# Plain fp32 matmuls in place of three fp32r products, in a chain of four attention layers

## The chip, the core and the metric

The kernel runs on one core of a Trainium2 chip. The metric is the device time of one execution in microseconds (us); the time before is the median of three runs.

## The reference

The input x and a context have 32 batches of 64 tokens (rows) by 256. Four blocks follow each other, all in fp32:

```python
# layer 0: softmax over the 256 columns, 8 heads, contraction over the 64 rows
xn  = (x - mean) * rsqrt(var + eps) * gamma + beta          # per batch
out = x + Wo @ attention(Wq @ xn, Wkv @ context) + bo
# layer 1: 16 heads of 16, keys and values from layernorm(context), queries from x
x   = x + tanh(gate) * (attention(x @ Wq.T, a @ Wk.T, a @ Wv.T) @ Wo.T)
# layer 2: queries from x, keys and values from [context, x]; 128 keys
h   = rmsnorm(attention(x @ q_w + q_b, [ctx, x] @ kv_w + kv_b) @ out_w + out_b + x, w)
x   = x + gelu(h @ mlp_w1 + mlp_b1) @ mlp_w2 + mlp_b2        # 256 -> 1024 -> 256
# layer 3: self attention, cross attention with the context, MLP, each after a layernorm
x   = x + attention(ln(x) @ w_qkv + b_qkv, mask) @ w_ao + b_ao
x   = x + attention(ln(x) @ w_q + b_q, ctx @ w_kv + b_kv, mask) @ w_co + b_co
x   = x + gelu(ln(x) @ w1 + b1) @ w2 + b2
```

## The kernel before

**Layer 0** is a loop of 64 iterations (a pair of batches and two heads each), written out by hand: scores `sc`, softmax, transposes `pt`, values `av`. TensorE works here on row-tiled and column-tiled plain fp32 matmuls; its weights are folded beforehand and no projection of the kind below occurs. At fixed places of an iteration `fill` (line 1138) puts in instructions from lists that `chain` (1128) has recorded: constants, masks, the preparation of weights (`load_unit`, 503), and at the end `boot_steps` (1415), which does the first projections of layer 1 for two groups and the operands of a third. `fill` takes from a list only while the iteration's allowance for the engine lasts, and `boot_steps` is recorded once layer 1's weight units are through. Lists that are not empty when the loop ends are run out after it.

**Layers 1 to 3** work on groups of four batches (256 tokens as two tiles of 128), eight groups. In the code they are l = 0 to 3, since layer 3's self and cross attention count separately. For each group a layer has steps: normalise (`ln_stats`, `ln_apply`), turn to features by tokens (`to_fm`, 907), keys (`k_out`), values (`v_out`), queries (`fm_out`), attention in sets of 128 tokens (`attend`, 1388, with `a_scores` to `a_fin`), output projection (`out_add`), and the MLP (`mlp_steps`, 1279). Each step has a due time. All instructions are recorded, and then the class `Plan` orders them: `cost` (194) gives each instruction a time, `order` (289) is a list scheduler that starts, engine by engine, what can start first by those costs, with due times and a seeded random number for ties. The result fixes the order on each engine: TensorE (T), VectorE (V), ScalarE (A), GpSimd (G) and SyncE's DMA queue (S). The profile therefore shows nearly all instructions of layers 1 to 3 on line 125 (where the plan writes them) and those of layer 0 on line 156; tiles tell them apart.

**The split products.** A projection multiplies 256 features by 256 columns. Weights and operands are kept as two fp32r tiles each, a high part (the value cast to fp32r) and a low part (value minus high part). `terms` (925) lists the products; `proj_f` (928) and `proj_t` (934) issue them, with the weights or the tokens stationary:

```python
    def terms(w, x):
        return [(w[0], x[0], k) for k in range(2)] + [(w[0], x[1], k) for k in range(2)] + [(w[1], x[0], k) for k in range(2)]
```

So one 128x128 by 256 term takes three fp32r matmuls. The names in the profile: `xTh` and `xTl` are high and low parts of a turned operand, with a letter behind for its use (`a` tiles that `boot_steps` uses too, `o` attention output, `h` MLP hidden, `n` MLP input); `w` is a prepared weight, `wraw` and parts of `boot` are raw weights, `u` the gelu's output. Who makes them: `to_fm` casts the transposes on ScalarE and subtracts on VectorE; the MLP's hidden tile goes gelu to `u`, cast on ScalarE, subtraction on VectorE; `a_fin` (1089) makes attention output, in layer 3 with a multiplication on VectorE, a cast on ScalarE and a subtraction on GpSimd; context tiles are loaded raw (`ctx_steps`, 1229), cast on ScalarE, subtracted on GpSimd; `load_unit` loads a raw weight by DMA, scales its rows on GpSimd where a norm's scale is folded in, casts on ScalarE and subtracts on GpSimd (in a few cases VectorE).

A split weight takes twice the room, so there are 14 slots and layer 3's weights go into slots whose earlier weights are through; `load_at` (1576) says at which attention set each load comes. The bias rows (`bias_row`, 544) are the one place with plain fp32 matmuls on the whole array and 256 columns (tile `bb`).

Of the kernel before, what the change touches and what calls it, by code (L numbers as in the profile page):

```python
# [10 lines left out]
F32R = mybir.dt.float32r  # L11
# [15 lines left out]
NW = 12  # L27
NE = 3
BIG = 1.0e30


def f32(ap):
    return ap.bitcast(F32) if ap.dtype == F32R else ap

# [59 lines left out]
class Plan:  # L94
# [5 lines left out]
    SEED, TIE = 4, 0.5  # L100
# [93 lines left out]
    def cost(self, o):  # L194
# [4 lines left out]
        if o.key == "T":  # L199
            if o.method == "transpose":  # L200
                return 0.11, 0.25, (1, 1)
            l, r = ins[0], ins[1]
            k_, m_ = l.shape[0], self.size(l)
            rows = 4 if k_ <= 32 else 2 if k_ <= 64 else 1
            cols = 4 if m_ <= 32 else 2 if m_ <= 64 else 1
            n_ = self.size(r)
            if l.dtype == F32:
                return max(n_ * 1.67e-3, 0.1 if rows * cols == 1 else 0) / (rows * cols), 0.3, (rows, cols)
            return max(n_ * 0.418e-3, 0.12 if rows * cols == 1 else 0) / (rows * cols), 0.25, (rows, cols)
# [199 lines left out]
def mk_kernel(ctx: ExitStack, tc: tile.TileContext, a: dict, out: bass.AP):  # L409
# [16 lines left out]
    wraw = pool("wraw", 2)  # L426
# [13 lines left out]
    def wt(shape, dt, tag, bufs=2):  # L440
        if cur["boot"]:
            if tag == "kfm":
                return boot[:, 1024:1536].rearrange("p (k t) -> p k t", t=P)
            if cur["second"] == 2 and tag in ahead:
                return plan.tile(cur["w"], "w", shape, dt, tag, nm(tag), 2)
            o = {"xTh": 0, "xTl": 512, "qfm": 1536 - 512 * cur["second"], "craw": 2048, "z": 2048}.get(tag)
            if o is None:
                return plan.lazy(lambda: small.tile(shape, dt, tag=tag + "b", name=nm(tag), bufs=1), shape, dt)
            v = (bootx if dt == F32R else boot)[:, o:o + 512]
            return v.rearrange("p (k t) -> p k t", k=2)  # L450
        return plan.tile(cur["w"], "w", shape, dt, tag, nm(tag), bufs)
# [37 lines left out]
    ahead = {t: [ct([P, 2, D], F32R, f"{t}a{i}") for i in range(2)] for t in ("xTh", "xTl")}  # L489
    wraws = [t.rearrange("p (k n) -> p k n", k=2) for t in (boot[:, 1024:1536], boot[:, 1536:2048])]  # L490
    cur["raws"], cur["rawn"] = 2, 0
# [7 lines left out]
    def split(hi, lo, src):  # L499
        V.tensor_copy(hi, src)  # L500
        V.tensor_tensor(lo, src, f32(hi), ALU.subtract)

    def load_unit(w, key, slot, ap, rows=None, mul=None, biases=(), then=None):

        cur["rawn"] += 1
        if cur["raws"] == 2 or cur["rawn"] % 2:
            raw = plan.tile(wraw, "r", [P, 2, D], F32, "wraw", nm("wraw"), 2)
        else:
            raw = wraws[cur["rawn"] // 2 % (cur["raws"] - 2)]
        SY.dma_start(raw, ap.rearrange("(k p) n -> p k n", p=P))  # L510
        yield
        for fn in biases:
            fn(raw)
        t = plan.tile(wpool if slot < NW else cur["w"], "ww", [P, 2, 2, D], F32R, f"w{slot}", nm("w"), 1)
        if rows is not None:
            for k in range(2):
                G.tensor_scalar(raw[:, k], raw[:, k], rows[:, k:k + 1], None, ALU.mult)
        elif mul is not None:
            G.tensor_scalar(raw, raw, mul, None, ALU.mult)
        A.copy(t[:, 0], raw)  # L520
        (V if slot < 4 and plan.on else G).tensor_tensor(t[:, 1], raw, f32(t[:, 0]), ALU.subtract)
        w[key] = (t[:, 0], t[:, 1])
        if then:
            then()
        yield
# [67 lines left out]
    bootx = c0([P, 1024], F32R, "bootx")  # L593
# [75 lines left out]
    def weights1(w):  # L669
        return [load_unit(w, "k", 0, a["L1_WkT"], rows=g1, biases=[bias_f(bk1, vec("L1_ln_beta"))]),  # L670
                load_unit(w, "v", 1, a["L1_WvT"], rows=g1, biases=[bias_f(bv1, vec("L1_ln_beta"))]),
                load_unit(w, "q", 2, a["L1_WqT"], mul=0.25),
# [3 lines left out]
    def weights2(w):  # L676
        return [load_unit(w, "k", 4, a["L2_wk"]), load_unit(w, "v", 5, a["L2_wv"]),
                load_unit(w, "q", 6, a["L2_q_w"], mul=1.0 / 16, then=lambda: G.tensor_scalar(bq2, vec("L2_q_b"), 1.0 / 16, None, ALU.mult)),
                load_unit(w, "o", 7, a["L2_out_w"], biases=[bias_row(row2, vec("L2_bv"), a["L2_out_b"])])]

    def weights2m(w):
        return [load_unit(w, f"1{j}", 8 + j, a["L2_mlp_w1"][:, j * D:(j + 1) * D], rows=vec("L2_postnorm_w")) for j in range(4)] + \
               [load_unit(w, f"2{j}", (12, 13, 2, 3)[j], a["L2_mlp_w2"][j * D:(j + 1) * D], then=(lambda: spread_row(row2m, a["L2_mlp_b2"])) if j == 0 else None)
# [4 lines left out]
    s1q, s2q = ct([P, 2], F32, "s1q"), ct([P, 2], F32, "s2q")  # L688

    def quarter(dst, src):  # L690
        G.tensor_scalar(dst, src, 0.25, None, ALU.mult)
        return dst

    def weights3s(w):
        return [load_unit(w, "k", 0, a["L3_wk"], rows=s1, biases=[bias_f(bk3, sb1, vec("L3_bk"))]),
                load_unit(w, "v", 1, a["L3_wv"], rows=s1, biases=[bias_f(bv3, sb1, vec("L3_bv"))]),
                load_unit(w, "q", 4, a["L3_wq"], rows=quarter(s1q, s1), biases=[bias_f(bq3, sb1, vec("L3_bq"))],
                          then=lambda: V.tensor_scalar(bq3, bq3, 0.25, None, ALU.mult)),
                load_unit(w, "o", 6, a["L3_w_ao"], biases=[bias_row(row3a, bv3, a["L3_b_ao"])])]

    def weights3c(w):
        return [load_unit(w, "k", 5, a["L3_wkc"]), load_unit(w, "v", 7, a["L3_wvc"]),
                load_unit(w, "q", 8, a["L3_w_q"], rows=quarter(s2q, vec("L3_ln2_s")), biases=[bias_f(bq3c, vec("L3_ln2_b"), vec("L3_b_q"))],
                          then=lambda: V.tensor_scalar(bq3c, bq3c, 0.25, None, ALU.mult)),
                load_unit(w, "o", 9, a["L3_w_co"], biases=[bias_row(row3c, vec("L3_bvc"), a["L3_b_co"])])]

    def weights3m(w):
        return [load_unit(w, f"1{j}", 10 + j, a["L3_w1"][:, j * D:(j + 1) * D], rows=vec("L3_ln3_s"),
                          biases=[bias_f(b13[:, 2 * j:2 * j + 2], vec("L3_ln3_b"), vec("L3_b1")[:, 2 * j:2 * j + 2])]) for j in range(4)] + \
               [load_unit(w, f"2{j}", j, a["L3_w2"][j * D:(j + 1) * D], then=(lambda: spread_row(row3m, a["L3_b2"])) if j == 0 else None)  # L710
# [196 lines left out]
    def to_fm(x, tag=""):  # L907
# [5 lines left out]
        hi, lo = fm_tiles(tag)  # L913
        hf, lf = hi.rearrange("p k t -> p (k t)"), lo.rearrange("p k t -> p (k t)")
        A.copy(hf, p_)
        V.tensor_tensor(lf, p_, f32(hf), ALU.subtract)
        return (hi, lo)

    def fm_tiles(t=""):
        n = {"": 4, "o": 2, "h": 2, "n": 1}[t]  # L920
        hi = wt([P, 2, D], F32R, "xTh" + t, n)
        lo = wt([P, 2, D], F32R, "xTl" + t, n)
        return hi, lo

    def terms(w, x):
        return [(w[0], x[0], k) for k in range(2)] + [(w[0], x[1], k) for k in range(2)] + [(w[1], x[0], k) for k in range(2)]

    def proj_f(w, x, oc, p_):

        tt = terms(w, x)  # L930
        for i, (ww, xx, k) in enumerate(tt):
            mm(p_, ww[:, k, oc * P:(oc + 1) * P], xx[:, k, :], i == 0, i == len(tt) - 1)

    def proj_t(w, x, i, p_, first=True, last=True):

        tt = terms(w, x)
        for j, (ww, xx, k) in enumerate(tt):
            mm(p_, xx[:, k, i * P:(i + 1) * P], ww[:, k, :], first and j == 0, last and j == len(tt) - 1)

    def fm_out(w, x, tag, bias=None):  # L940
# [4 lines left out]
        for oc in range(2):  # L945
            put(o[:, oc], p_[:, oc * D:(oc + 1) * D], bias and bias[:, oc:oc + 1])
        return o

    def put(d, s_, bias):
        if bias is None:  # L950
            A.copy(d, s_)
        else:
            A.activation(d, s_, AF.Identity, bias=bias)
# [135 lines left out]
    def a_fin(u):  # L1089
        st, i = u["st"], u["i"]  # L1090
        if i == 0 and u["s"] == 0:
            st["o"] = fm_tiles("o")
        o_ = u["at"]
        c = slice(u["s"], u["s"] + 1) if u["two"] else slice(0, 2)
        hv, lv = [t[:, c, i * P:(i + 1) * P] for t in st["o"]]
        ov = o_[:, 0:D].rearrange("p (c t) -> p c t", c=2)[:, c]
        if u["kind"] == "k":
            A.copy(hv, ov)
            V.tensor_tensor(lv, ov, f32(hv), ALU.subtract)
        else:  # L1100
            rb = wt([P, 2, P], F32, "rb", 2)
            A.copy(rb.rearrange("p c t -> p (c t)"), o_[:, D:2 * D])
            V.tensor_tensor(rb, ov, rb, ALU.mult)
            A.copy(hv, rb)
            G.tensor_tensor(lv, rb, f32(hv), ALU.subtract)
# [123 lines left out]
    def ctx_steps(l, g, due, src=()):  # L1229
# [3 lines left out]
        def fetch():  # L1233
            st["raw"] = wt([P, 2, D], F32, "craw", 1)
            SY.dma_start(st["raw"], a["ctxT"][:, g * D:(g + 1) * D].rearrange("(k p) t -> p k t", p=P))

        def split_():
            hi, lo = fm_tiles()
            A.copy(hi, st["raw"])
            G.tensor_tensor(lo, st["raw"], f32(hi), ALU.subtract)  # L1240
            st["c"] = (hi, lo)
        step(n + "a", due - 2, fetch, *src)
        step(n, due, split_, n + "a")
# [21 lines left out]
    def query_step(l, g, key, w, bias, row, due):  # L1265
        st = grp[l, g]

        def fn():
            st["q"] = fm_out(w["q"], st[key], "qfm", bias)
# [9 lines left out]
    def mlp_steps(l, g, w, b1, row, key, dues, out_=None):  # L1279
# [3 lines left out]
        def up(j):  # L1283
# [5 lines left out]
            t = wt([P, 2, D], F32, "u", 3)  # L1289
            for c in range(2):  # L1290
                A.activation(t[:, c], p_[:, c * D:(c + 1) * D], AF.Gelu_apprx_tanh, bias=b1[:, j * 2 + c:j * 2 + c + 1])
            st[f"h{j}"] = fm_tiles("h")
            hh, hl = st[f"h{j}"]
            A.copy(hh, t)
            V.tensor_tensor(hl, t, f32(hh), ALU.subtract)
# [20 lines left out]
    for l in range(4):  # L1316
        for g in range(NG):
# [8 lines left out]
            elif l == 1:  # L1326
# [6 lines left out]
                query_step(l, g, "x", w2, bq2, None, f - 2)  # L1333
# [117 lines left out]
    for k in range(NP + 2):  # L1451
# [4 lines left out]
        if k == 2:  # L1456
# [3 lines left out]
            later = weights2m(w2)  # L1460
            units += later[:4]
# [106 lines left out]
    for t, tiles in ahead.items():  # L1568
        tiles += [cur["w"].tile([P, 2, D], F32R, tag=f"{t}_{i}", name=f"{t}_{i}", bufs=1) for i in range(2)]
# [11 lines left out]
    load_at(7, later[4:6])  # L1581
    load_at(16, later[6:7])
    load_at(22, later[7:])
# [10 lines left out]
    for n in range(NS):  # L1594
        if n == 4:
            cur["raws"] = 4
# [73 lines left out]
```

## Time and profile before

| | |
|---|---|
| median of three runs | 1142.94 us (1140.23 to 1143.46) |
| the profiled execution | 1139.34 us |
| its span, first to last instruction | 1137.6 us |
| mean granted TensorE clock | 0.98 |
| instructions | 35727 |
| HBM | 26.30 MB read, 2.10 MB written, 25 GB/s over the span |

Times are microseconds. PE is TensorE's matmuls and PEld its weight loads, which overlap them; DVE is VectorE, ACT ScalarE, POOL GpSimd, SP SyncE, which issues DMAs. The ends of matmuls are modelled and overlap, so how fast they follow each other is read from their starts. A group line has: source line, engine, operation, tile written and tiles read, shapes, number of instructions, busy time, mean ns of one, then the idle time of the engine before them and what ended it. A wait is put down to the releaser that came last.

### The profile page before, as it was taken

Reading aid. Unit: us, or ns where it says so; the run is one execution under the profiler, and the core shown is the slowest. Engines: PE = TensorE matmul, PEld = TensorE weight load, DVE = VectorE, ACT = ScalarE, POOL = GpSimd, SP = SyncE. Lnnn points to the kernel's source line nnn. Section 1 sums busy time; section 2 is a strip of 40 time slices with the busy share of each in tenths; the row PEclk is TensorE's granted clock in tenths of the full one; section 3 lists DMA queues with packets and bytes.
Section 4 is the critical chain, followed back from the end, with each engine's and each line's share of the span. In section 5 each row is a group of like instructions: output and inputs, shape, how many; then the busy total and the mean of one; then the engine's idle time right before and its main releaser. Section 6 shows DMA issues by size and latency. Waiting matters only on the chain.

```text
span 1137.6 us, 35727 instructions
## 1 busy us (share of the span) xinstructions
PE 1064.6 (94%) x14396; PEld 872.7 (77%) x14396; DVE 861.2 (76%) x1485; ACT 909.2 (80%) x2326; POOL 783.1 (69%) x919
## 2 busy tenths in 40 slices
PE   6999999999999996699999999999999989889998
PEld 4666666666666664588988989998998868779998
DVE  3778888787888872678788977777878888777842
ACT  2888888888888984477778888889898787878974
POOL 3789888888888864546545554457866999996520
PEclk9999999999999998799999999999999998989999
DMA  3001111111011000211211100001000111110000
GB/s 96 20 24 39 41 38 34 34 34 35 27 37 33 26 20 29 88 49 39 79 51 44 36 27 28 22 11 39 21 20 20 48 51 51 42 33 22 11 20 29
DMA packets 41301, 41.22 MB, mean 36 GB/s; under 512 B 7059, under 2 KB 37796, under 8 KB 41136
## 3 DMA queue, kind: packets, MB, share of 16 engines
q1 hardware_dynamic: 40816, 38.54, 10.9%
q8 instruction: 114, 1.87, 0.7%
q10 hardware_dynamic: 320, 0.40, 0.1%
q14 instruction: 51, 0.42, 0.1%
HBM read 26.30 MB, written 2.10 MB: 25 GB/s over the span
## 4 chain that ended last, share of the span: by engine, by line
PE 42%; POOL 8%; DVE 5%; ACT 2%; issue 1%; DVEq 0%; POOLq 0%; ACTq 0%
PE pj L125 39%; PE s L125 4%; POOL E L125 3%; DVE E L125 2%; DVE mx L125 1%; POOL xTlo L125 1%; POOL xTl L125 1%; ACT PTe L125 1%; DVE sm L125 1%; POOL boot L125 1%; POOL w L125 1%; POOL x L125 1%; POOL wraw L125 0%; ACT L125 0%; POOL rstda L125 0%
## 5 line engine op out<-in xcount | busy, mean ns | idle before, releaser
L156 POOL TENSOR_TENSOR E<-E,rs 128x512 f32<-128x512 f32 x256 | 263.2, 1042 | 51.7 <-DVE rs L156 46.7
L156 ACT ACTIVATE E<-sc,mx 128x256 f32<-128x256 f32 x512 | 237.9, 479 | 11.8 <-DVE rs L156 11.1
L156 DVE TENSOR_REDUCE mx<-sc 128x4 f32<-128x1024 f32 x128 | 156.3, 1221 | 6.6 <-PE sc L156 2.6
L156 PE MATMUL sc<-cd,T 64*128 64x256 f32 x1024 | 143.7, 400 | 11.7 <-ACT E L156 11.1
L125 POOL TENSOR_TENSOR E<-E,sm 128x512 f32<-128x512 f32 x96 | 101.2, 1079 | 68.5 <-DVE sm L125 55.8
L156 PE MATMUL av<-PT,us 128*64 128x256 f32 x1024 | 125.2, 385 | 0.3 <-DVE PT L156 0.3
L156 PEld LDWEIGHTS av<-PT,us 128*64 128x64 f32 x1024 | 68.1, 136 | 60.3 <-issue 21.0
L156 PEld LDWEIGHTS pt<-ident,E 64*128 64x128 f32 x2048 | 83.3, 139 | 37.4 <-POOL E L156 20.1
L156 PEld LDWEIGHTS sc<-cd,T 64*128 64x128 f32 x1024 | 89.2, 189 | 27.7 <-ACT E L156 19.8
L125 DVE TENSOR_REDUCE sm<-E 128x16 f32<-128x1024 f32 (+1 forms) x80 | 96.0, 1200 | 16.1 <-ACT E L125 16.0
L156 ACT ACTIVATION_READ_ACCUMULATOR E<-sc,mx 128x1 f32 x512 | 106.7, 208 | 0.0
L125 ACT COPY PTe<-pj 128x512 f32<-128x512 f32 x160 | 88.0, 590 | 17.7 <-PE pj L125 15.6
L125 PE MATMUL pj<-ident,E 128*128 128x128 f32 x640 | 90.3, 279 | 9.0 <-ACT E L125 3.2
L156 PE MATMUL pt<-ident,E 64*128 64x64 f32 x2048 | 94.7, 227 | 3.3 <-ACT PT L156 1.0
L125 PE MATMUL pj<-w,xThh 128*128 128x256 f32 x512 | 93.4, 287 | 0.1
L156 DVE COPY PT<-pt 128x512 f32<-128x512 f32 x128 | 86.7, 678 | 8.5 <-PE pt L156 7.8
L156 ACT COPY PT<-pt 128x512 f32<-128x512 f32 x128 | 75.3, 588 | 22.2 <-PE pt L156 21.0
L125 PE MATMUL pj<-xThn,w 128*128 128x256 f32 x512 | 92.3, 286 | 0.7 <-DVE rb L125 0.4
L156 DVE RECIPROCAL rs<-sm 128x2 f32<-128x2 f32 x256 | 40.7, 159 | 64.3 <-ACT E L156 60.1
L125 ACT ACTIVATE E<-E 128x1024 f32<-128x1024 f32 x80 | 84.9, 1062 | 5.4 <-DVE E L125 4.2
L125 PEld LDWEIGHTS pj<-ident,E 128*128 128x128 f32 x640 | 71.0, 142 | 17.7 <-ACT E L125 3.7
L125 DVE TENSOR_TENSOR xTlh<-u,xThh 128x512 fp32r<-128x512 f32 x64 | 54.2, 850 | 30.5 <-ACT xThh L125 30.2
(229 smaller groups left out, 2782.5 us busy)
## 6 DMA issues: line engine op xcount, KB each, us to landing
kb<-kfm SPq DMA_DIRECT2D x44, 128.0 KB, 2.0
xd<-in_x SPq DMA_DIRECT2D x32, 128.0 KB, 2.9
cd<-in_ctx SPq DMA_DIRECT2D x32, 128.0 KB, 2.7
boot<-in_ctxT SPq DMA_DIRECT2D x16, 256.0 KB, 2.9
kb<-kfm SPq DMA_DIRECT2D x64, 64.0 KB, 1.9
xt<-in_x SPq DMA_DIRECT2D x16, 128.0 KB, 2.0
boot<-in_ctx SPq DMA_DIRECT2D x8, 256.0 KB, 2.7
out<-x SPq DMA_DIRECT2D x8, 256.0 KB, 2.1
```

The source lines that it names most:

```text
L125: getattr(self.engines[o.key], o.method)(*[real(x) for x in o.p], **{k: real(x) for k, x in o.k.items()})
L156: return f(*p, **k)
```

## The change

Weights and operands stay plain fp32. `proj_f` and `proj_t` issue one fp32 matmul for each term; high and low parts, their casts and subtractions, and the raw tiles are gone. Scalings that were folded into weights (1/4 and 1/16 for the queries) move to the activation that evicts the queries. `to_fm` copies on VectorE. All weights have slots of their own; layer 2's eight MLP units are all prepared in layer 0's chains, so its four later loads go. Operand tiles get more buffers, the softmax tile `E` four in place of three. The planner's costs for matmuls and its seed change, so that the order on every engine is another.

```diff
-NW = 12
-NE = 3
+NE = 4
...
-    SEED, TIE = 4, 0.5
+    SEED, TIE = 0, 0.5
...
-            if l.dtype == F32:
-                return max(n_ * 1.67e-3, 0.1 if rows * cols == 1 else 0) / (rows * cols), 0.3, (rows, cols)
-            return max(n_ * 0.418e-3, 0.12 if rows * cols == 1 else 0) / (rows * cols), 0.25, (rows, cols)
+            if rows * cols == 1:
+                return max(n_ * (0.85e-3 if l.dtype == F32 else 0.418e-3), 0.11), 0.3, (1, 1)
+            return n_ * (1.3e-3 if l.dtype == F32 else 0.418e-3) / (rows * cols), 0.3, (rows, cols)
...
-    def load_unit(w, key, slot, ap, rows=None, mul=None, biases=(), then=None):
-
-        cur["rawn"] += 1
-        if cur["raws"] == 2 or cur["rawn"] % 2:
-            raw = plan.tile(wraw, "r", [P, 2, D], F32, "wraw", nm("wraw"), 2)
-        else:
-            raw = wraws[cur["rawn"] // 2 % (cur["raws"] - 2)]
-        SY.dma_start(raw, ap.rearrange("(k p) n -> p k n", p=P))
+    def load_unit(w, key, slot, ap, rows=None, biases=(), then=None):
+
+        t = plan.tile(wpool if slot < 24 else cur["w"], "ww", [P, 2, D], F32, f"w{slot}", nm("w"), 1)
+        SY.dma_start(t, ap.rearrange("(k p) n -> p k n", p=P))
         yield
...
-        A.copy(t[:, 0], raw)
-        (V if slot < 4 and plan.on else G).tensor_tensor(t[:, 1], raw, f32(t[:, 0]), ALU.subtract)
-        w[key] = (t[:, 0], t[:, 1])
+        w[key] = t
...
-        hi, lo = fm_tiles(tag)
-        hf, lf = hi.rearrange("p k t -> p (k t)"), lo.rearrange("p k t -> p (k t)")
-        A.copy(hf, p_)
-        V.tensor_tensor(lf, p_, f32(hf), ALU.subtract)
-        return (hi, lo)
+        t = fm_tile(tag)
+        V.tensor_copy(t.rearrange("p k t -> p (k t)"), p_)
+        return t
+
+    def fm_tile(t=""):
+        return wt([P, 2, D], F32, "xT" + t, {"": 5, "o": 3, "h": 4, "n": 2}[t])
...
     def proj_f(w, x, oc, p_):
 
-        tt = terms(w, x)
-        for i, (ww, xx, k) in enumerate(tt):
-            mm(p_, ww[:, k, oc * P:(oc + 1) * P], xx[:, k, :], i == 0, i == len(tt) - 1)
+        for k in range(2):
+            mm(p_, w[:, k, oc * P:(oc + 1) * P], x[:, k, :], k == 0, k == 1)
...
         if u["kind"] == "k":
-            A.copy(hv, ov)
-            V.tensor_tensor(lv, ov, f32(hv), ALU.subtract)
+            A.copy(to, ov)
         else:
             rb = wt([P, 2, P], F32, "rb", 2)
             A.copy(rb.rearrange("p c t -> p (c t)"), o_[:, D:2 * D])
-            V.tensor_tensor(rb, ov, rb, ALU.mult)
-            A.copy(hv, rb)
-            G.tensor_tensor(lv, rb, f32(hv), ALU.subtract)
+            V.tensor_tensor(to, ov, rb, ALU.mult)
...
         def fetch():
-            st["raw"] = wt([P, 2, D], F32, "craw", 1)
-            SY.dma_start(st["raw"], a["ctxT"][:, g * D:(g + 1) * D].rearrange("(k p) t -> p k t", p=P))
-
-        def split_():
-            hi, lo = fm_tiles()
-            A.copy(hi, st["raw"])
-            G.tensor_tensor(lo, st["raw"], f32(hi), ALU.subtract)
-            st["c"] = (hi, lo)
-        step(n + "a", due - 2, fetch, *src)
-        step(n, due, split_, n + "a")
+            st["c"] = fm_tile()
+            SY.dma_start(st["c"], a["ctxT"][:, g * D:(g + 1) * D].rearrange("(k p) t -> p k t", p=P))
+        step(n, due - 2, fetch, *src)
...
-            t = wt([P, 2, D], F32, "u", 3)
+            st[f"h{j}"] = t = fm_tile("h")
             for c in range(2):
                 A.activation(t[:, c], p_[:, c * D:(c + 1) * D], AF.Gelu_apprx_tanh, bias=b1[:, j * 2 + c:j * 2 + c + 1])
-            st[f"h{j}"] = fm_tiles("h")
-            hh, hl = st[f"h{j}"]
-            A.copy(hh, t)
-            V.tensor_tensor(hl, t, f32(hh), ALU.subtract)
...
-            later = weights2m(w2)
-            units += later[:4]
+            units += weights2m(w2)
...
-    load_at(7, later[4:6])
-    load_at(16, later[6:7])
-    load_at(22, later[7:])
     load_at(26, g3[:2], 2)
     load_at(43, g3[2:], 2)
```

## The prediction

> **What bounds the kernel now.** I read the page's first part, then a cut of the span into stages, then the order of TensorE's matmuls in two short stretches. The page names TensorE (PE), but its busy time is modelled from overlapping matmuls, so I checked it by the starts.
>
> ```profile
> PE 1064.6 (94%) x14396; PEld 872.7 (77%) x14396; DVE 861.2 (76%) x1485; ACT 909.2 (80%) x2326; POOL 783.1 (69%) x919
> ```
>
> The cut has five stages: layer 0's loop; the stretch from its last matmul to layer 1's first scores; the main part; the stretch in which layer 3's weights come in; the end. Columns: window, its length, busy PE, weight loads, DVE, ACT, POOL, then the granted clock, DMA share, GB/s.
>
> ```profile
> 0.00:437.90 437.90, 412.78 (x4520) 279.85 (x4520) 337.32 (x709) 361.32 (x1238) 351.59 (x473) 1.00 0.12 36
> 437.90:464.50 26.60, 12.52 (x70) 9.86 (x69) 6.71 (x16) 9.01 (x19) 10.76 (x17) 0.80 0.11 37
> 464.50:880.00 415.50, 403.06 (x6752) 364.81 (x6753) 334.99 (x480) 343.21 (x675) 241.33 (x252) 0.98 0.12 38
> 880.00:1000.00 120.00, 105.22 (x1536) 93.39 (x1532) 95.97 (x161) 93.62 (x198) 113.94 (x111) 0.93 0.16 50
> 1000.00:1137.60 137.60, 130.96 (x1531) 124.82 (x1530) 86.21 (x120) 102.00 (x197) 65.50 (x68) 0.98 0.07 22
> ```
>
> PE is idle for 12.4, 14.8 and 6.6 us in the last three stages, 34 of 673 us: it sets their length, except from 880 to 1000, where POOL is busy for 114 of 120. In the second stage nobody is busy: it is a chain of waits. The same cut for PE instructions that read a prepared weight tile gives the number of split products by stage:
>
> ```profile
> 0.00:437.90 437.90, 3.38 (x24) 1.00 0.12 36
> 437.90:464.50 26.60, 8.61 (x48) 0.80 0.11 37
> 464.50:880.00 415.50, 257.67 (x1920) 0.98 0.12 38
> 880.00:1000.00 120.00, 61.59 (x419) 0.93 0.16 50
> 1000.00:1137.60 137.60, 108.83 (x855) 0.98 0.07 22
> ```
>
> That is 3264 but for two counted on both sides of a cut, as the code has it: 34 projections of 256x256 weights against a group's 256 tokens (4 in layer 1, 14 in layer 2, 16 in layer 3), eight groups, four terms of 128x128 weights by 256 columns in each: 1088 terms, each done in three products.
>
> **The price of one term, before and after.** The timeline of PE (start, time until the last one's end, what, how many) has both kinds at full clock:
>
> ```profile
> 599.49 0.40 PE L125 MATMUL pj<-w,xTh 128*128 128x256 f32 x2
> ...
> 602.82 0.40 PE L125 MATMUL pj<-w,xTho 128*128 128x256 f32 x2
> ```
>
> Between these starts lie 28 fp32r matmuls in 3.33 us: 0.119 us each, 0.357 a term. The new form, plain fp32 on the whole array with 256 columns, is in the kernel already, in the bias rows:
>
> ```profile
> 766.49 1.03 PE L125 MATMUL pj<-boot,bb 128*128 128x256 f32 x4
> 767.45 0.69 PE L125 MATMUL pj<-rr,ones 1*128 1x256 f32 x2
> ```
>
> The code issues two matmuls here and the trace has four records: a plain fp32 matmul runs as two. One alone takes 0.38 us (mean of its group), four take 1.03, so the starts are (1.03 - 0.38) / 3 = 0.217 apart, and a term costs 0.433. The change adds 0.076 us to each term.
>
> The Trainium skill ("FP8 and Floating Point Precision", TensorE Precision Notes) counts true fp32 as four passes of the array. By passes alone a term would go from three to four, an estimate of 0.476 us and +130 us over all terms. The rows give 0.433 to 0.357, a ratio of 1.21, and +83; they decide.
>
> **Part by part.**
>
> Layer 0 (437.9 us). The ratio of busy to length after the first 40 us is 385 of 398, so what goes onto PE here lengthens it. Built, the changed program has all preparation of layer 1's first groups (boot_steps) ahead of the last layer-0 matmul; before, 24 of its 72 products were there. PE gets 24 terms x 0.433 = 10.4 us less 24 x 0.119 = 2.9, and 20 more transposes at 0.11 (four in 0.60 us with 0.27 for the last): +9.7. The cause is that no weight is split in the chains of fill: per unit one ACT cast (0.62) and one POOL subtraction (1.27) go. What is moved in takes more than matmuls: the stretch's 9.0 us of ACT, 6.7 of DVE and 10.8 of POOL, which go to engines that idle for 77, 101 and 86 us in the loop, and the DMAs of context tiles and keys on SP's queue, between layer 0's own loads, which are issued one step of four iterations ahead. All of it lies beside PE and I count it at nothing, as I do the four added units, DMAs alone; both programs give SP 293 DMAs. I take +10; bounds 0 (hidden in the 25 us that PE idles) to +15 (some wait for ACT or DVE within an iteration).
>
> The stretch between (26.6 us). Its matmuls are now in layer 0, and so are its waits:
>
> ```profile
> 446.26 0.47 PE L125 MATMUL pt<-ident,boot 128*128 128x128 f32 x1 [4.72 <-ACT boot L125]
> 448.75 0.90 PE L125 MATMUL pt<-ident,boot 128*128 128x128 f32 x3 [2.02 <-ACT boot L125]
> 457.48 0.50 PE L125 MATMUL pt<-bootx,w 128*128 128x256 f32 x2 [1.94 <-ACT bootx L125]
> 464.50 0.33 PE L125 MATMUL s<-mrow,ind 4*64 4x128 bf16 x8 [1.56 <-DVE xTla L125]
> ```
>
> What stays is the draining of layer 0's last bank by DVE and the change of PSUM pools. The nearest row is the last wait, 1.6 us with the transposes before it done at 462.9; I take 3 us, bounds 2 to 12 (a chain that still ends late). So -23.6, bounds -24.6 to -15.
>
> The rest (673 us). PE: 1920 / 3 x 0.076 = +48.6, 419 / 3 x 0.076 = +10.6, 855 / 3 x 0.076 = +21.7: +80.9 on the engine that sets the end. Tile modes change as often (561 runs of one kind of matmul after layer 0 before, 536 after), so that part is nil.
>
> Off PE much goes:
>
> ```profile
> L125 DVE TENSOR_TENSOR xTlh<-u,xThh 128x512 fp32r<-128x512 f32 x64 | 54.2, 850 | 30.5 <-ACT xThh L125 30.2
> L125 ACT CAST xThh<-u 128x512 fp32r<-128x512 f32 x64 | 39.4, 622 | 6.7 <-ACT u L125 3.0 <-PE pj L125 1.5 <-ACT xThn L125 1.1
> L125 POOL TENSOR_TENSOR xTlo<-rb,xTho 128x256 fp32r<-128x256 f32 x32 | 28.5, 890 | 21.4 <-ACT xTho L125 18.3 <-DVE sm L125 3.1
> L125 POOL TENSOR_TENSOR w<-wraw,w 128x512 fp32r<-128x512 f32 x18 | 22.9, 1274 | 17.7 <-ACT w L125 17.7
> ```
>
> By these and the smaller rows ACT loses 115 us of casts (xThh 39.4, w 19.8, xTha 15.6, xTho 13.1 and four small), DVE 78 of subtractions (xTlh, xTlo 15.6, w 8.6) and POOL 86 (xTlo, w 32.1, xTl 22.3, a scaling 3.0); the 56 turns cost DVE a copy (0.67) where it had a subtraction (0.68). Off the bounding engine this is worth only PE's idle time. From 880 to 1000 POOL loses 28 us (10.2 xTl, 11.7 xTlo, 6.4 w) and needs 86; PE needs 105.2 + 10.6 = 116, so the stretch becomes PE's own and about 11 of its 14.8 idle us go. Of the 12.4 and 6.6 I take 7 and 3: shorter hand-offs (gelu writes the operand itself, a context tile is loaded where it is used, a resident weight doesn't wait for its slot's last reader, a fourth softmax tile E). The clock lost 2%, 7% and 2% in the three stages, 19.5 us of full clock, in spells after idle stretches; I take 5 back. Together -26, bounds 0 to -53. What is late next is PE itself. The planner prices a full-array fp32 matmul of 256 columns at 0.218 us, half of the row: it will think PE free when it isn't, but its orders hold for each engine whatever the times, and longer matmuls give the others more time; counted at nothing, against 0 to +15.
>
> Sum: +10 - 23.6 + 80.9 - 26 = +41. The profiled execution took 1139.3 (span 1137.6), so 1180.6; the median of the runs lies 3.6 above that execution, so 1184.
>
> **Rivals.**
>
> A: nothing comes back but the stretch between, because PE's idle time is latency of the softmax chains and the planner, sure that PE is half free, lines up work that PE reaches late. Then +10 to +15, -20 and +81: 1139.3 + 71 to 76 + 3.6 = 1214 to 1219, and up to 1230 with the planner's loss. For it: from 464 to 880 no other engine is over 83% busy and PE idles all the same. Against: POOL's 114 of 120.
>
> B, faster: a plain fp32 term in a long stream costs what the planner's new line says, 0.218, its two records overlapping. Then PE loses 1064 x 0.139 = 148 us after layer 0: 1139.3 + 4 - 23.6 - 148 + 3.6 = 975, with PE's 34 idle us kept. DVE and ACT still need some 435 us each in what would be 525, so waits would grow: 975 to 1050. It decides at 0.393 us a term (1088 x 0.036 = 39 us, the 23.6 + 26 less 10 that the rest gives): records 0.197 apart. Against: 0.217 between all records of the row, the same for a pair of row-tiled fp32 matmuls with 256 columns (eight records in 0.97 us, two at a time, 0.24 a pair).
>
> C: all idle time and clock comes back and layer 0 hides its share: 80.9 - 53 - 24.6 + 0 = +3, 1146: no change that can be measured, or just slower. It needs every wait after layer 0 to have been one for a split; the waits for softmax sums and maxima say no.
>
> **How the numbers follow.** Forecast 0.70, A 0.20, B 0.04, C 0.04, and 0.02 for a change that the program doesn't carry out as said (the built program has 2176 matmuls fewer, 3264 against 1088, so hardly). Range: from between C and the forecast to A's middle, 1158 to 1218; all unknown terms at their ends together give 1146 and 1239. A measurement of this kernel tells about 0.3% from no change. Faster 0.05, same 0.02, slower 0.93.
>
> **What would show it.** Right: 2176 records of plain fp32 in the projections, 0.217 apart; PE busier than 97% after layer 0 (95% before); the first scores within 5 us of layer 0's last matmul, which comes some 10 us later; ACT, DVE and POOL below 65% after it; half-clock spells nearly gone. Wrong: records at 0.2 or less; idle PE of over 40 us after layer 0, waiting for PSUM banks or for an engine that stands behind a late matmul; a late end of boot_steps.

## The result, and the profile after

The changed kernel takes 1214.97 us (median of four runs, 1213.63 to 1216.46) against 1141.59 for the kernel before in the same comparison (1139.29 to 1143.46): a ratio of 1.064, 95% interval 1.062 to 1.067. The profiled execution took 1213.63 us with a span of 1211.8. The forecast was 1184 in a range of 1158 to 1218: the sign was right, and the time lies at the range's upper end, where rival A had put it (1214 to 1219). The range reached so far only because its end had been set at A's middle; the forecast's own sum misses the time by 31 us.

First the line of busy times, as before:

```profile
PE 1146.5 (95%) x13308; PEld 882.5 (73%) x13308; DVE 790.3 (65%) x1365; ACT 805.1 (66%) x2122; POOL 690.9 (57%) x843
```

PE went from 1064.6 to 1146.5 us, and every other engine lost work: DVE 71, ACT 104, POOL 92. The cut into stages, with the same columns (window, length, busy PE, weight loads, DVE, ACT, POOL, clock, DMA share, GB/s):

```profile
0.00:453.70 453.70, 428.96 (x4566) 290.05 (x4567) 343.82 (x725) 361.49 (x1239) 344.58 (x474) 1.00 0.14 41
453.70:870.00 416.30, 400.86 (x5526) 329.82 (x5525) 259.91 (x353) 252.13 (x503) 183.37 (x207) 0.98 0.11 35
870.00:990.00 120.00, 112.64 (x1354) 92.50 (x1346) 80.70 (x120) 74.82 (x157) 74.69 (x66) 1.00 0.09 29
990.00:1080.00 90.00, 77.75 (x964) 61.93 (x964) 65.77 (x102) 58.43 (x113) 57.86 (x63) 0.94 0.08 25
1080.00:1211.80 131.80, 126.30 (x922) 108.18 (x910) 40.12 (x67) 58.25 (x112) 30.44 (x34) 0.99 0.05 17
```

There is no stretch between any more. Layer 0 ends 15.8 us later, and the main part, from layer 1's first scores to the end, went from 673.1 to 757.6 us. PE is idle in it for 40 us, more than the 34 before, though no other engine is over 74% busy in any of its windows; from 990 to 1080 PE idles for 12 of 90 us and the clock is at 0.94. The end of layer 0 in the timeline of PE:

```profile
451.37 2.30 PE L150 MATMUL av<-PT,us 128*64 128x256 f32 x16
454.24 0.26 PE L119 MATMUL s<-mrow,ind 4*64 4x128 bf16 x8 [0.58 <-DVE x L150]
...
455.12 1.99 PE L119 MATMUL pj<-xTa,w 128*128 128x256 f32 x8
456.95 1.89 PE L119 MATMUL pj<-w,xTa 128*128 128x256 f32 x8
458.68 1.89 PE L119 MATMUL pj<-xTa,w 128*128 128x256 f32 x8
```

The first scores come 0.6 us behind layer 0's last matmul, where it was 26.6. The starts of the last two rows lie 1.73 us apart with eight records in between: 0.216 each, 0.432 a term. The groups of the page that are new:

```profile
L119 PE MATMUL pj<-xTn,w 128*128 128x256 f32 x512 | 122.0, 386 | 2.1 <-DVE xTn L119 1.0
L119 PE MATMUL pj<-w,xTh 128*128 128x256 f32 x512 | 122.2, 386 | 0.0
L119 ACT COPY PTe<-pj 128x512 f32<-128x512 f32 x160 | 88.6, 588 | 70.0 <-PE pj L119 65.5
```

All groups of this kind together hold 2176 records, two for each of 1088 terms; 48 of them are in layer 0. The cut for PE instructions that read a prepared weight, for the main part as a whole (2128 records of projections, the others are for biases):

```profile
454.24:1211.80 757.56, 509.14 (x2200) 0.98 0.09 30
```

Before, its three stages held 428.1 us of such work. The last row of the groups is a first sign of where time went: ACT stood for 65.5 us ahead of these evictions waiting for PE, and the waits of PE in the main part (total, times, longest) name the same eviction first:

```profile
PE pj L119 <- ACT PTe L119: 8.7, 17, 1.2
PE s L119 <- DVE E L119: 5.7, 5, 2.6
PE pj L119 <- ACT E L119: 5.4, 5, 1.9
PE pj L119 <- DVE xTo L119: 4.3, 5, 1.8
```

Before, the waits for PTe came to 3.8 us. The two engines wait for each other, although ACT is busy for only 59% of the main part.

### The profile page after: what moved, and what is told of

It is laid out like the page before. It is cut to its first block, busy times and chain, and to the rows that moved or that the text cites. A ratio compares the mean times of both kernels' runs of the same rounds, so it can differ in the third digit from the quotient of the medians.

```text
span 1211.8 us, 33203 instructions
## 1 busy us (share of the span) xinstructions
PE 1146.5 (95%) x13308; PEld 882.5 (73%) x13308; DVE 790.3 (65%) x1365; ACT 805.1 (66%) x2122; POOL 690.9 (57%) x843
## 3 DMA queue, kind: packets, MB, share of 16 engines
q1 hardware_dynamic: 40816, 38.54, 10.2%
## 4 chain that ended last, share of the span: by engine, by line
PE 76%; ACT 12%; DVE 7%; issue 3%; POOL 2%; DMA 0%; SPq 0%; ACTq 0%; POOLq 0%; DVEq 0%
PE pj L119 49%; PE pt L150 8%; PE av L150 7%; PE sc L150 5%; ACT E L150 5%; PE s L119 4%; ACT PT L150 3%; DVE E L119 2%; PE pt L119 2%; POOL E L150 1%; ACT PTe L119 1%; DVE mx L119 1%; ACT E L119 1%; DVE mx L150 1%; DVE PT L150 1%
## 5 line engine op out<-in xcount | busy, mean ns | idle before, releaser
L119 POOL TENSOR_TENSOR E<-E,sm 128x512 f32<-128x512 f32 x96 | 97.9, 1044 | 108.0 <-DVE sm L119 74.4
L119 ACT COPY PTe<-pj 128x512 f32<-128x512 f32 x160 | 88.6, 588 | 70.0 <-PE pj L119 65.5
L119 PE MATMUL pj<-xTn,w 128*128 128x256 f32 x512 | 122.0, 386 | 2.1 <-DVE xTn L119 1.0
L119 PE MATMUL pj<-w,xTh 128*128 128x256 f32 x512 | 122.2, 386 | 0.0
L119 PEld LDWEIGHTS pj<-xTn,w 128*128 128x128 f32 x512 | 95.8, 192 | 16.2 <-DVE xTn L119 1.3
L119 PEld LDWEIGHTS pj<-w,xTh 128*128 128x128 f32 x512 | 97.0, 193 | 13.9 <-issue 0.5
L150 DVE COPY PT<-pt 128x512 f32<-128x512 f32 x128 | 86.9, 679 | 18.9 <-PE pt L150 17.7
L119 DVE TENSOR_REDUCE mx<-s 128x8 f32<-128x1024 f32 (+1 forms) x48 | 58.6, 1222 | 51.8 <-PE s L119 51.5
```

The lines of the kernel that those rows point to most:

```text
L119: getattr(self.engines[o.key], o.method)(*[real(x) for x in o.p], **{k: real(x) for k, x in o.k.items()})
L150: return f(*p, **k)
```

## The experiments

The question: the term of the sum for what comes back was -26, and the main part gave nothing back. Three theories were set against each other: that the planner, which prices a full-array fp32 matmul of 256 columns at 0.218 us, half of the 0.432 that the trace shows, lines up work that PE reaches late (theory 1); that the idle time is latency of the softmax chains, whatever the planner believes (theory 2); and that the new order is only an unlucky draw of the planner's seed (theory 3). "Main part" means first scores to the end throughout; the half-clock time is summed from the trace's clock records.

**The price put right.** One number is changed; the instructions stay, their order moves.

```diff
-                return max(n_ * (0.85e-3 if l.dtype == F32 else 0.418e-3), 0.11), 0.3, (1, 1)
+                return max(n_ * (1.69e-3 if l.dtype == F32 else 0.418e-3), 0.11), 0.3, (1, 1)
```

> The changed kernel with one number altered: the planner's price of a plain fp32 matmul of 256 columns on the whole array is 0.433 us (1.69e-3 a column), what its records take, in place of 0.218. Theory 1 (the misprice makes the planner line up work that TensorE reaches late, so TensorE's 41 us of idle time after layer 0 stay): idle time falls below 25 us, 1185 to 1200 us. Theory 2 (the idle time is latency of the softmax chains and doesn't depend on the price): 1208 to 1222 us, idle time still about 40.

Measured: 1174.86 us, ratio to before 1.030 (1.029 to 1.032): 40 us less than the changed kernel, more than the theory of the price had asked for. The cut of this kernel and its waits in the main part:

```profile
0.00:453.20 453.20, 427.74 (x4566) 289.16 (x4567) 343.65 (x725) 361.95 (x1239) 345.12 (x474) 1.00 0.14 41
453.20:870.00 416.80, 409.28 (x5709) 337.43 (x5716) 269.22 (x371) 286.02 (x546) 191.08 (x218) 1.00 0.11 35
870.00:990.00 120.00, 119.45 (x1541) 99.21 (x1533) 98.39 (x151) 81.33 (x166) 84.61 (x76) 1.00 0.11 37
990.00:1170.50 180.50, 173.25 (x1506) 147.04 (x1504) 79.25 (x120) 94.93 (x184) 67.07 (x76) 1.00 0.06 20
```

```profile
PE pj L119 <- ACT PTe L119: 3.4, 5, 1.3
PE pj L119 <- POOL E L119: 2.5, 2, 2.1
PE pj L119 <- DVE xTo L119: 1.8, 1, 1.8
PE s L119 <- DVE E L119: 0.8, 2, 0.6
```

Layer 0 is as it was; the whole gain, 757.6 to 716.7 us, is in the main part. PE's idle time there falls from 40.0 to 14.8 us and the time at half clock from 23.9 to 3.4; those are 25 us, and some 10 if all of that half-clock time was work; the other 5 or so of the gain were not traced. From 870 to 990 PE is busy for 119.45 of 120. So 25 of the changed kernel's 40 us of idle time are made by the order and not by the chains' latency.

**The seed**, in the changed kernel, in the one with the right price, and in the kernel before with the changed kernel's seed:

```diff
-    SEED, TIE = 0, 0.5
+    SEED, TIE = 4, 0.5
```

> The changed kernel with the planner's seed of before (4) in place of 0, all else the same: how far ties alone move it. Theory 1 (price): within 8 us of 1215. Theory 3 (the seed was found for one kernel and a fresh draw loses): 1220 to 1240.

> The changed kernel with the true price of a plain fp32 matmul (0.433 us) and the seed of before (4): does the 40 us that the price gave hold for another draw of ties? Theory 1 (price): 1168 to 1188 us against 1218.6 with this seed and the low price. Rival (a lucky order): over 1200.

> The kernel before with the changed kernel's seed (0) in place of 4. If ties matter little: 1138 to 1150 us. Theory 3 (a seed found for that kernel): 1150 to 1170, so part of the 73 us would be the seed's.

Measured: 1218.59 us (ratio 1.069, 1.068 to 1.071) against 1214.97; 1176.54 (1.031, 1.028 to 1.033) against 1174.86; and the kernel before with seed 0 at 1155.09 (1.014, 1.012 to 1.016). A draw moves the fp32 kernel by 2 to 4 us, a tenth of what the price does. The kernel before is another matter: its seed is worth 15 us, so part of what one reads as the cost of the change may be a good draw on the other side; two seeds cannot say which of them is the usual one. With seed 0 on both sides the gap is 60 us, with seed 4 it is 78.

**The same mistake in the kernel before.** Its fp32r products are priced rightly at 0.12 us; here they are priced at half.

```diff
-            return max(n_ * 0.418e-3, 0.12 if rows * cols == 1 else 0) / (rows * cols), 0.25, (rows, cols)
+            return max(n_ * 0.235e-3, 0.06 if rows * cols == 1 else 0) / (rows * cols), 0.25, (rows, cols)
```

> The kernel before with its planner's price of an fp32r matmul of 256 columns halved, 0.06 us in place of 0.12, nothing else: the same misprice, turned on the kernel whose price was right. Theory 1: slower by 20 to 50 us, 1160 to 1190, with TensorE idle for over 55 us after layer 0's loop and the stretch behind it. Rival (only the fp32 kernel is touchy): 1138 to 1155.

Measured: 1208.32 us, ratio 1.060 (1.058 to 1.062), more than expected. The main part goes from 673.1 to 740.7, PE's idle time in it from 34 to 81, the half-clock time from 34 to 68. Its waits, and those of the same kinds in the kernel before:

```profile
PE pj L125 <- ACT PTe L125: 13.7, 27, 1.5
PE s L125 <- DVE E L125: 8.7, 7, 2.6
PE pj L125 <- ACT E L125: 7.8, 7, 2.1
```

```profile
PE pj L125 <- ACT PTe L125: 3.8, 6, 1.2
...
PE pj L125 <- ACT E L125: 3.2, 2, 2.9
...
PE s L125 <- DVE E L125: 2.6, 4, 1.0
```

They are the three that lead in the changed kernel too, in the same order. A half price does this with both forms of the matmuls.

**A price too high**, 1.5 times the row:

```diff
-                return max(n_ * (0.85e-3 if l.dtype == F32 else 0.418e-3), 0.11), 0.3, (1, 1)
+                return max(n_ * (2.54e-3 if l.dtype == F32 else 0.418e-3), 0.11), 0.3, (1, 1)
```

> The changed kernel with the price of a plain fp32 matmul of 256 columns set 1.5 times too high (0.65 us). Theory 1 in its general form (what counts is that the planner knows TensorE to be the bound): 1170 to 1185 us, like the true price. If only the true price will do: over 1195, half of the loss of the price that is half.

Measured: 1215.41 us, ratio 1.067 (1.063 to 1.070). It loses as much as the half price, against the expectation. PE idles for 42.0 us of the main part, but for other releasers:

```profile
PE pj L119 <- ACT E L119: 10.7, 12, 2.0
PE pj L119 <- ACT xTh L119: 6.0, 9, 1.3
PE pj L119 <- POOL E L119: 5.7, 11, 2.1
```

Now PE comes to the transposes of `E` before the softmax is done with it. The trace shows the same as a distance: for each of the 80 sets of scores in layers 1 to 3, the time on PE from the set's last scores to its first transposes. Its median is 14.9 us before and 19.0 with the fp32r products at half price; in the fp32 kernel it is 23.2 at half price, 13.4 at the right one and 10.1 at 1.5 times. So a set is in flight for longer as the price is lower. With too short a flight the wait is plain: PE stands before `E`. How too long a flight makes PE wait was tried in one way:

**Is it the tiles that a set holds?** A set in flight holds an `E`; six tiles at half price, and three at the right one:

```diff
-NE = 4
+NE = 6
```

> The changed kernel, low price kept, with six softmax tiles E in place of four. In its trace 22 us of TensorE's work lie between a set's scores and its transposes (median), against 13.5 with the true price, so every set holds its tile E and its place longer. Theory 1a (the low price costs time because the sets in flight use up the tiles E): with six tiles 1180 to 1200 us and idle TensorE below 28 us. Theory 1b (it is the order on the other engines, whose instructions stand behind matmuls that come late): 1205 to 1222.

> The changed kernel with the true price (1174.9 us) and three tiles E as before the change in place of four. Theory 1a: with 13.5 us in flight three tiles are nearly enough, 1175 to 1185 us. If the fourth tile is what made the price worth 40 us: 1195 or more.

Measured: 1211.02 us (1.062, 1.060 to 1.064) and 1174.92 (1.030, 1.028 to 1.032). The number of tiles is not what stalls the changed kernel (with six PE still idles for 39.9 us, and the flight even grows to 25.6), and at the right price the fourth tile, which the change adds, is worth nothing. What is left is that DVE and ACT, whose order the plan fixes, stand behind evictions of matmuls that PE reaches late. The traces fit this: from 455 us on, ACT waits for matmuls of PE for 142 us in all at 1.5 times the price, 196 at the right price and 267 at half, and DVE for 182, 190 and 261. That these waits are what in turn holds PE is argued, not shown.

**The splits alone.** In the kernel before, no low parts are made: the high part stands in for the low one, the three products stay. So PE issues the matmuls that it did, and the other engines lose casts and subtractions. The attention outputs, context tiles and MLP hidden tiles are treated alike.

```diff
-        hi, lo = fm_tiles(tag)
...
-        A.copy(hf, p_)
-        V.tensor_tensor(lf, p_, f32(hf), ALU.subtract)
-        return (hi, lo)
+        V.tensor_copy(hi.rearrange("p k t -> p (k t)"), p_)
+        return (hi, hi)
...
-        (V if slot < 4 and plan.on else G).tensor_tensor(t[:, 1], raw, f32(t[:, 0]), ALU.subtract)
-        w[key] = (t[:, 0], t[:, 1])
+        w[key] = (t[:, 0], t[:, 0])
```

> The kernel before with its three fp32r products for each term, but the low parts are neither made nor read: the high part stands in for them, gelu and the attention output are written as fp32r at once, and the turns are copied on VectorE. So the other engines are relieved as in the change, and TensorE's work stays (the low parts are left out of the computation). If the others' work costs nothing but what TensorE waits for: after the first scores 640 to 665 us (before 673), and the whole gains another 10 to 15 from the stretch before them, 1108 to 1135 us. If the splits pace the kernel: under 1090.

Measured: 1109.43 us, ratio 0.973 (0.971 to 0.975). Its main part:

```profile
452.80:1107.00 654.20, 629.09 (x9808) 577.83 (x9807) 443.83 (x640) 485.34 (x937) 348.91 (x369) 0.98 0.11 37
```

Taking 73 us off DVE, 53 off ACT and 72 off POOL is worth 18.9 us in the main part: 8.7 of them are idle time of PE, and the rest is its busy time, with some 14 us less at half clock. The first scores come at 452.8 us in place of 464.5, so taking the splits away is enough to let layer 1's first steps move into layer 0. With this the main part's +84.5 us comes apart: -18.9 for the splits (654.2 for 673.1), +62.5 for the form of the matmuls at the right price (716.7 for 654.2), +40.9 for the price. The first two are loose: between their kernels the seed and the number of tiles `E` differ too, and the kernel before has 688.8 in place of 673.1 with seed 0. The planner's price of row- and column-tiled fp32 matmuls, which the change lowers from 1.67 to 1.3 ns a column (divided by the number of tiles), was not tried by itself.

**Layer 1's first steps kept behind layer 0**, in the changed kernel:

```diff
-        if k > 2 and boots is None and all(len(b) <= n for b, n in zip(both, w1_left)):
+        if k > 59 and boots is None and all(len(b) <= n for b, n in zip(both, w1_left)):
```

> The changed kernel with boot_steps recorded only at iteration 60 of layer 0's loop, so that it runs after the loop as it did before; the plan's part is unchanged. If moving it in was worth the waits less TensorE's work: layer 0 ends 12 to 16 us earlier (438 to 442), the stretch behind it grows from 0.6 to 20 to 28 us, and the whole is slower by 5 to 14 us, 1220 to 1229. If it was worth nothing: 1212 to 1218.

Measured: 1221.79 us, ratio 1.071 (1.068 to 1.073), 7 us over the changed kernel. The stretch is back, and the timeline shows its chain:

```profile
445.13 1.97 PE L119 MATMUL pt<-bootx,w 128*128 128x256 f32 x8 [1.74 <-DVE bootx L119]
448.33 0.33 PE L119 MATMUL pt<-ident,boot 128*128 128x128 f32 x1 [1.23 <-ACT boot L119]
...
457.73 1.97 PE L119 MATMUL pt<-bootx,w 128*128 128x256 f32 x8 [1.74 <-DVE bootx L119]
...
463.40 0.26 PE L119 MATMUL s<-mrow,ind 4*64 4x128 bf16 x8 [0.94 <-DVE xTa L119]
```

Layer 0 ends at 437.9, where it ended before, and the first scores are at 463.4 for 454.3. So the move brings the first scores 9 us forward: the stretch is 25 us shorter, and layer 0 is 15.8 us longer. The main parts are equal (756.6 and 757.6).

**One pass for a term.** Two kernels bound what the matmuls can still give, both with less precise operands. The first is the changed kernel, whose projections read the upper 16 bits of each fp32 number as bf16 and leave out the rest; it keeps the order.

```diff
+        if k.pop("one", False):
+            p[1:] = [x.bitcast(BF16)[:, 1::2] for x in p[1:]]
```

> The changed kernel, order and tiles the same, but each projection term reads only the upper half of its fp32 numbers as bf16, so it is one record of about 0.11 us and not two of 0.216; the lower halves are left out of the computation. If TensorE's work sets the length after layer 0 (758 us): 1064 x 0.32 = 340 us leave it, and the stage falls to 480 to 560 us, bounded by VectorE's and ScalarE's 445 us and by waits; whole 935 to 1020 us. If latency sets it: over 1080 us.

The second is the kernel without low parts, with one product of high parts instead of three, so that operands are rounded to fp32r.

```diff
-        return [(w[0], x[0], k) for k in range(2)] + [(w[0], x[1], k) for k in range(2)] + [(w[1], x[0], k) for k in range(2)]
+        return [(w[0], x[0], k) for k in range(2)]
```

> A version that drops the terms with low parts: one fp32r product for each term, priced right (0.12 us), operands rounded to fp32r and nothing more. Two products of three leave TensorE: 2128 x 0.119 = 253 us after layer 0, from 629 us to some 375, so VectorE's and ScalarE's 440 to 485 us set the rest: main stage 490 to 545 us, whole 945 to 1000 us. If TensorE was not what set the length: over 1060.

Measured: 974.2 us (one run) and 1031.32 us (ratio 0.904, 0.902 to 0.906; the expectation missed it). Their main parts:

```profile
448.10:972.40 524.30, 409.63 (x7678) 306.40 (x7677) 443.28 (x639) 436.08 (x883) 348.01 (x369) 0.93 0.13 42
```

```profile
448.40:1030.70 582.30, 453.97 (x7680) 375.29 (x7679) 445.16 (x640) 454.47 (x913) 349.87 (x369) 0.85 0.12 41
```

In both PE is no longer the bound: DVE, ACT and PE have about the same work, all wait for each other, and PE idles for 115 and 128 us. Both are faster than the kernel before, but neither keeps its operands; of the kernels that keep them none is.

## Why the prediction was right, and where its sum was not

**The price of a term: right.** Records are 0.216 us apart, a term takes 0.432 (0.433). PE's busy time in the main part rose by 78.3 us for the +80.9 of the sum, and by some 83 without the gain of about 5 that 10 us less of half clock made. Rival B needed records at 0.197 or less, and falls.

**Layer 0: mis-sized.** +15.8 us for +10, just over the bound of 15. Six iterations of the loop with eight records of a projection each took 8.08 us in place of 6.16, 1.92 where eight records are 1.73: 11.5 us for 48 records, where the 24 products of before had lengthened two iterations by 3.3 us. Six iterations with transposes alone took 0.6 to 0.8 longer each, 4 us together. Some 3 us are left, in what was counted at nothing: iterations 18 to 35, in which weights are filled, took 121.3 us for 112.6 before. Part of that is only a move, since the bias rows' matmuls, which lengthen an iteration by 0.6 to 1.1 us in both kernels, run around iterations 15 to 31 now and ran around 44 to 59 before. The kernel with the late first steps has 119.4 us there, and its layer 0 still ends at 437.9, as before, though the 3.3 us of products are not in it; which instruction costs the 3 us was not traced.

**The stretch between: right.** 0.6 us for the 3 that were taken. It and layer 0 come to -10.2 together (the forecast had -13.6).

**What comes back, and the planner: the step that failed.** The sum took -26 for idle time and clock, and the planner's wrong price "counted at nothing, against 0 to +15", because "its orders hold for each engine whatever the times, and longer matmuls give the others more time". The first experiment measures that term: +40.9 in the main part. It took away all that would have come back, so that the changed kernel idles more (40.0 us for 33.9) and spends 24 us at half clock. With the price put right the step before it in the sum holds: the main part is 716.7 us, where the forecast's terms give 673.1 + 80.9 - 26 = 728 (what came back is then 37 us, not 26), PE is busy for 97.9% of it (97% was the sign given), the half-clock time is nearly gone, and the window at 870 is PE's own, as was read from POOL's 114 of 120 before. The reason given for "nothing" was wrong: an order does hold on each engine, but it was made for times that are not so, and engines then wait at their places in it. The trace of before could have said so only in part; an order's sensitivity to its prices isn't in any row of a single kernel. The nearest evidence was in the diff: the new price is half of the row, and the line that it replaces had 1.67 ns a column, 0.428 us for 256, close to the 0.432 measured.

**Rival A: right in number and in one of its two reasons.** Nothing came back, and the planner's price is why; that its work lines up behind a late PE fits the waits of ACT and DVE. Its other reason, that the idle time is latency of softmax chains, falls with the first experiment: the chains are the same there and PE idles for 14.8 us. The sum for A left the planner's loss as something on top of it (up to 1230); in fact the loss stands in place of what would have come back.

**Signs.** 2176 records, 0.216 apart: as said. First scores within 5 us: as said. ACT, DVE and POOL below 65% after layer 0: 59, 59 and 46%. PE over 97% busy and half-clock spells nearly gone: not in the changed kernel (94.7%, five spells in the main part), but with the right price. The sign for "wrong", idle PE of over 40 us with waits for engines that stand behind late matmuls, is just met in its size, at 40.0; its waits are mostly for ACT and DVE, and that these stand behind late matmuls is argued above.

**Rival C**, 1146, needed all idle time back and layer 0 for nothing. Even with the right price PE idles for 14.8 us of the main part, and layer 0 took 15.8 us more: it falls on both.

## What to carry to other kernels

When an instruction changes its form under a planner that orders by prices, take the new price from the spacing of that form in a trace before anything else is judged: half of it and 1.5 times of it cost 40 us each here, more than half of what the whole change cost. Work taken off engines that don't set the end is worth little: some 200 us of casts and subtractions bought 19 us, by PE's idle time and half clock, and 1064 terms that got 0.076 us longer on PE, 80.9 us by the sum, took back three to four times as much. And compare orders over more than one seed before a few per cent are laid to an edit: one kernel moved by 15 us, another by 2 to 4.

## What the runs showed of the hardware

Half clock comes without a long idle stretch. In the changed kernel's main part the clock is halved in five spells, of 3.4 or 6.8 us, and the longest stretch in which PE is idle is 2.9 us. One such spell in the timeline:

```profile
1022.79 3.55 PE L119 MATMUL pj<-xTa,w 128*128 128x256 f32 x8 [2.92 <-DVE E L119]
1026.17 0.38 PE L119 MATMUL pj<-ident,rx 128*128 128x128 f32 x2
1026.49 0.65 PE L119 MATMUL pj<-PTe,vbd 128*32 128x64 f32 x32
1027.07 1.99 PE L119 MATMUL pj<-w,xTa 128*128 128x256 f32 x8
1028.90 1.89 PE L119 MATMUL pj<-xT,w 128*128 128x256 f32 x8
```

Eight records take 3.38 us to the next start here, and 1.83 at 1027.07. The Trainium skill ("TensorE: Matmul & The Clock Gate", Part 1: The HAM clock gate) has the clock halved after an idle window of about 3.4 us. The spells' lengths agree with such windows: all are 3.4 us or two to four times that (3.4, 6.8, 10.2, once 13.7) in these runs, but for those that the end of a run cuts. The idle stretches do not: shorter ones are enough. In the kernel without low parts the clock is halved in three spells of 20 us together, and PE is never idle for more than 1.7 us at a time in its main part. Where PE had too little to do, the kernel with one fp32r product, it ran at half clock for 173 us of 582, in 30 spells, with only two idle stretches of 3.4 us or more; the kernel with one bf16 pass, whose order had been priced at 0.218 us a matmul, had 75 us of half clock. But idle time alone doesn't do it either: with the price 1.5 times too high PE idles for 42 us of the main part in short waits and has one spell, where the half price has 40 us and five. So neither the longest idle stretch nor the sum decides, and by which rule the clock is set no run here tells.
